# Experts' input of the last five blocks: block transposes on VectorE and a trip through DRAM in place of TensorE transposes

## The chip, the cores and the metric

The kernel runs on one core of one Trainium2 chip. The metric is device time of one execution in microseconds (us). The kernel before takes 1170.67 us (median of 3 runs, 1169.65 to 1171.47). The engines are named as in the profile: PE (TensorE), DVE (VectorE), ACT (ScalarE), POOL (GpSimd), SP (SyncE, whose queue issues every DMA here).

## The reference

The input x is 4096 tokens of 512 features, float32. Two sublayers follow, each of them `x + layernorm(f(layernorm(x)))`.

- Attention over 64 fixed latent keys: `Q = h Wq^T + bq` in 16 heads of 32; for each head and token 64 logits against the latent keys; the four largest go through a softmax and weight the latent vectors; `V = h Wv^T + bv` is added; the sum goes through `Wo` and `bo`. (K is computed by the reference and not used.)
- Experts: `up = h Wu^T`, `gate = h Wg^T`, `hidden = silu(up) * gate` (2048 wide), `out = hidden Wd^T`. The three matrices are ternary: each weight is rounded to -1, 0 or 1 times a scale of its matrix.

## The kernel before

**Tiling.** Tokens are taken in 8 blocks (b = 0 to 7) of 512, a block in 4 tiles (t) of 128 tokens. Features lie in 4 chunks (c or k) of 128. The 2048 expert columns are 16 chunks (e = 0 to 15) of 128; a loop over e within a loop over b is the frame of the whole kernel, and "chunk" below means one turn e of it.

**One chunk on PE.** `F.up("u", e)` (8 matmuls into the PSUM tile pu, line 676), `F.up("g", e)` (8 matmuls into pg, line 676), then `F.down(e - 1)` (8 matmuls into the four accumulators acc, line 719). In chunk 0 the down of the block before (chunk 15) stands in that place. Each expert matmul is done twice, on a high and a low part of the activations: the high part `hi` is the float32 value rounded to the type FP32R, the low part `lo` is what is left. The weights are ternary and exact. PSUM holds one pu and one pg.

**One chunk on ACT and DVE.** ACT: tanh of pu (line 685). DVE: silu (688). DVE: gate, h times pg (693). ACT: hi (704). DVE: lo (709), which `F.down(e)` of the next chunk reads with hi.

**The pieces in between.** While block b's experts run, the attention of block b + 1 is computed in pieces. `pieces(A, after)` writes by hand in which chunk and place each piece is emitted: `put(e, k, f, ...)`, where place 3 is between up-u and tanh, 0 between tanh and silu, 1 between up-g and gate, 2 between down(e - 1) and lo. The scheduler is off (`tc.manual_schedule()`), so each engine runs its instructions in just this order. `after` is the attention of block b + 2, whose input is prepared at the end of block b.

The pieces of a block's attention A, in the kernel before:

- `a_stats`, `a_rstd`, `a_apply` (chunks 10 and 11): first layernorm, on the tiles `xa` loaded by `load_normed` in chunk 6. `a_blocks(c)` (11, place 2): for each feature chunk c, four DVE transposes of 128x128 (line 317; DVE's transpose turns each 32x32 square by itself) into a tile `za`, and a DMA to the DRAM tile `da` (321). `a_load` (15, place 2): four DMAs from `da` to `hT` (326), which put the squares where a full transpose would have them. In `hT` the tokens of each square row are in the order (c t i).
- `q` (chunks 1, 2, 4, 6; line 344), `l` (logits, 358), `m` (top 8, 376), `r` (384 to 388), `e` (exp, 393), `n` (399 to 404), `z` (transpose of the weights through DRAM, 411 to 419), `v` and `y` (431, 448), `o` (459), `o_bias`, `o_rstd`, `o_apply` (chunks 11 to 13): attention itself. q and v read `hT` through `taken(k)` and `ordered(k)`, patterns that pick tokens in the order they need.
- `f_stats`, `f_rstd` (13), `f_apply` (14): second layernorm, on DVE and POOL. `f_trans(t)` (tiles 0 and 1 at chunk 14 place 1, tiles 2 and 3 at chunk 15 place 0): `transpose_row` (282) does four PE transposes of 128x128 against `ident` into PSUM; ACT copies the result to `self.hi`, named hT_f (496); DVE subtracts it to give `self.lo`, named lT_f (497). These two are the operands `parts` of `Experts(b + 1)`: every up matmul reads all 512 tokens of one of them.

Buffers: hT, hT_f and the same of block b + 2 take turns in the place `X{b % 2}`; attnT and lT_f in `Y{b % 2}`. So `a_load` for block b + 2 waits until up-g of chunk 15 of block b has been read. Blocks 0 and 1 are prepared in a different way (class `FirstAttention`, with an order of its own at the start), block 2 (`SecondAttention`) with PE transposes for both layernorms' outputs.

At the end of a block: `y_stats` in chunk 0 of the next, `y_out` after silu of its chunk 1 (DVE, line 272, then POOL and the store).

Of the kernel before, what the change touches and what calls it, by code (L numbers as in the profile page):

```python
# [10 lines left out]
F32 = mybir.dt.float32  # L11
F32R = mybir.dt.float32r
BF16 = mybir.dt.bfloat16
AF = mybir.ActivationFunctionType
ALU = mybir.AluOpType
AX = mybir.AxisListType

P = 128
# [40 lines left out]
def latent_attention_ternary_glu(  # L59
# [15 lines left out]
    nc = tc.nc  # L75
    NT, D = x_in.shape
    E = wuT.shape[1]
    DC = D // P
    EC = E // P
    TB = 512  # L80
    TT = TB // P
# [5 lines left out]
    work = ctx.enter_context(tc.tile_pool(name="work", bufs=2))  # L87
    small = ctx.enter_context(tc.tile_pool(name="small", bufs=4))
    dram = ctx.enter_context(tc.tile_pool(name="dram", bufs=3, space=bass.MemoryType.DRAM))
# [16 lines left out]
    def transposed(which, b, name, dtype):  # L106
        return work.tile([P, DC, TB], dtype, tag=f"{which}{b % 2}", name=name, bufs=1)
# [7 lines left out]
    CH = E // 2  # L115
    halves = [(k, h) for k in range(DC) for h in range(2)]
    raw = {}
    late = []
    for q in range(DC):
        w = work.tile([P, D], F32, tag="xa", name=f"raw_d_6_{q}", bufs=TT)  # L120
        late.append(w)
    for n, i in RAW_ORDER:
        raw[n, i] = wpool.tile([P, CH], F32, tag="chunk", name=f"raw_{n}_{i}", bufs=6 * DC)
    for q in range(DC):
        raw["d", 6 + q] = late[q]
    count = {"u": 2 * DC, "g": 2 * DC, "d": 2 * DC + 2}

    def load_x(b):
# [8 lines left out]
    normed = {}  # L137

    def load_normed(b):
        for t in range(TT):  # L140
            xt = work.tile([P, D], F32, tag="xa", name=f"xa_{b}_{t}", bufs=TT)
            r = b * TB + t * P
            nc.sync.dma_start(out=xt, in_=x_in[r : r + P, :])
            normed[b, t] = xt

    def load_up(n, src):
        for i, (k, h) in enumerate(halves):
# [22 lines left out]
    for i in range(count["d"]):  # L170
        rows = 2 * P if i < 6 else P
        r = i * 2 * P if i < 6 else 12 * P + (i - 6) * P
# [21 lines left out]
    tern = {}  # L194
# [84 lines left out]
    def transpose_row(h, name):  # L279
        pt = at_psum(f"pt_{name}")  # L280
        for c in range(DC):
            nc.tensor.transpose(pt[:, c * P : (c + 1) * P], h[:, c * P : (c + 1) * P], ident)  # L282
        return pt.rearrange("p (c k) -> p c k", k=P)
# [3 lines left out]
    class Attention:  # L287
        def __init__(self, b):
            self.b = b
            self.hT = None  # L290
            self.attnT = None
            self.norm_a = Norm(f"a{b}")
            self.norm_o = Norm(f"o{b}")
            self.norm_f = Norm(f"f{b}")
            self.rows = {}
            self.qT, self.w, self.top, self.m8, self.left, self.wT, self.pv = ({} for _ in range(7))
            self.po = {}

        def a_stats(self, t):
            self.norm_a.stats(t, normed[self.b, t])

        def a_rstd(self, lo, hi):
            self.norm_a.rstd(lo, hi)

        def a_apply(self, t):
            self.norm_a.apply(normed[self.b, t], normed[self.b, t], t)

        def a_blocks(self, c):

            if c == 0:
                self.da = dram.tile([P, 4, DC, P], F32, tag="da", name=f"da_{self.b}", bufs=2)
            z = work.tile([P, 4, P], F32, tag="w", name=f"za_{self.b}_{c}", bufs=4)
            for t in range(TT):
                nc.vector.transpose(
                    z[:, :, 32 * t : 32 * t + 32],
                    normed[self.b, t][:, c * P : (c + 1) * P].rearrange("p (k j) -> p k j", j=32),
                )  # L320
            nc.sync.dma_start(out=self.da[:, :, c, :], in_=z)

        def a_load(self):
            self.hT = transposed("X", self.b, f"hT_{self.b}", F32)
            for k in range(4):
                nc.sync.dma_start(
                    out=self.hT[32 * k : 32 * k + 32, :, :],
                    in_=self.da.rearrange("(a j) k c e -> k j a (c e)", j=32)[k],
                )

        def taken(self, k):
            return self.hT.rearrange("p a (c e) -> p c a e", e=P)[:, k]

        def ordered(self, k):
            return self.hT.rearrange("p a (c t i) -> p c t a i", t=TT, i=32)[:, k]


        def q(self, c):  # L340
# [145 lines left out]
            self.rows["f", t] = row(f"h_f{self.b}_{t}")  # L486
            self.norm_f.apply(self.rows["f", t], x_tiles[self.b][t], t)

        def f_alloc(self):
            self.hi = transposed("X", self.b, f"hT_f{self.b}", F32R)  # L490
            self.lo = transposed("Y", self.b, f"lT_f{self.b}", F32R)

        def f_trans(self, t):
            src = transpose_row(self.rows.pop(("f", t)), f"f{self.b}_{t}")
            dst = self.hi[:, :, t * P : (t + 1) * P]
            nc.scalar.copy(dst, src)
            nc.vector.tensor_tensor(
                self.lo[:, :, t * P : (t + 1) * P], src, dst.bitcast(F32), ALU.subtract
            )

    class SecondAttention(Attention):
# [9 lines left out]
        def sorted(self, dst, src):  # L513
            return self.mixed(dst), src.rearrange("p (a t i) -> p a t i", t=TT, i=32)

        def a_apply(self, t):
            self.rows["a", t] = row(f"h_a{self.b}_{t}")
            self.norm_a.apply(self.rows["a", t], normed[self.b, t], t)

        def a_trans(self, t):  # L520
            if self.hT is None:
# [143 lines left out]
    class Experts:  # L665
# [6 lines left out]
        def up(self, n, e):  # L672
            p = ps_up.tile([P, TB], F32, tag=n, name=f"p{n}_{self.b}_{e}")
            for k in range(DC):
                for i, part in enumerate(self.parts):
                    nc.tensor.matmul(  # L676
                        p, lhsT=tern[n, 2 * k + e // 8][:, (e % 8) * P : (e % 8 + 1) * P], rhs=part[:, k, :],
                        start=(k == 0 and i == 0), stop=(k == DC - 1 and i == 1),
                    )
            (self.pu if n == "u" else self.pg)[e] = p  # L680
# [197 lines left out]
    def pieces(A, after):  # L878

        at = {(e, k): [] for e in range(EC) for k in range(4)}  # L880

        def put(e, k, f, *args):
            at[e, k].append(lambda: f(*args))

        if A.b > 1:
            if A.b == 2:
                put(0, 0, A.a_apply, 0)
                put(0, 0, A.a_apply, 1)
                put(0, 1, A.a_trans, 0)
                put(0, 1, A.a_trans, 1)  # L890
                put(0, 1, A.a_apply, 2)
                put(0, 1, A.a_apply, 3)
                put(0, 2, A.a_trans, 2)
                put(0, 2, A.a_trans, 3)
            put(1, 0, A.q, 0)
            put(2, 0, A.q, 1)
            put(4, 0, A.q, 2)
            put(6, 0, A.q, 3)
        put(1, 1, A.l, 0)
        put(2, 2, A.l, 1)  # L900
        put(5, 0, A.l, 2)
        put(7, 0, A.l, 3)
        for i in range(8):
            put(2 + i, 0, A.m, i)
            put(2 + i, 2, A.r, i)
            put(3 + i, 3, A.e, i)
            put(3 + i, 1, A.n, i)
            put(3 + i, 1, A.z, i)
        for c in range(DC):
            put(5 + 2 * c, 1, A.v, c)  # L910
            put(5 + 2 * c, 1, A.y, c)
        if after is not None and after.b == 2:
            put(14, 2, after.a_stats, 0)
            put(14, 2, after.a_stats, 1)
            put(15, 1, after.a_stats, 2)
            put(15, 1, after.a_stats, 3)
            put(15, 1, after.a_rstd, 0, 4)
        elif after is not None:
            put(10, 2, after.a_stats, 0)
            put(10, 2, after.a_stats, 1)  # L920
            put(11, 0, after.a_stats, 2)
            put(11, 0, after.a_stats, 3)
            put(11, 0, after.a_rstd, 0, TT)
            for t in range(TT):
                put(11, 1, after.a_apply, t)
            for c in range(DC):
                put(11, 2, after.a_blocks, c)
            put(15, 2, after.a_load)
        put(11, 2, A.o, 0)
        put(11, 2, A.o, 1)  # L930
        put(11, 2, A.o_bias, 0)
        put(12, 0, A.o, 2)
        put(12, 0, A.o_bias, 1)
        put(12, 0, A.o_rstd, 0, 2)
        put(12, 1, A.o, 3)
        put(12, 1, A.o_bias, 2)
        put(12, 2, A.o_apply, 0)
        put(12, 2, A.o_apply, 1)
        put(12, 2, A.o_bias, 3)
        put(12, 2, A.o_rstd, 2, 4)  # L940
        put(13, 0, A.o_apply, 2)
        put(13, 0, A.o_apply, 3)
        put(13, 1, A.f_stats, 0)
        put(13, 1, A.f_stats, 1)
        put(13, 1, A.f_rstd, 0, 2)
        put(13, 2, A.f_stats, 2)
        put(13, 2, A.f_stats, 3)
        put(13, 2, A.f_rstd, 2, 4)
        put(14, 0, A.f_apply, 0)
        put(14, 0, A.f_apply, 1)  # L950
        put(14, 1, A.f_alloc)
        put(14, 1, A.f_trans, 0)
        put(14, 1, A.f_trans, 1)
        put(14, 1, A.f_apply, 2)
        put(14, 1, A.f_apply, 3)
        put(15, 0, A.f_trans, 2)
        put(15, 0, A.f_trans, 3)
        return at

    prev = None  # L960
    for b in range(NB):
        if b > 0:
            A, nxt = nxt, after
        after = None
        F = Experts(b, (A.hi, A.lo))
        at = {}
        for e in range(EC):
            if e == 4 and 0 < b < NB - 1:
# [119 lines left out]
```

## Time and profile before

| | |
|---|---|
| median of 3 runs | 1170.67 us |
| the profiled execution | 1169.34 us |
| its span, first to last instruction | 1167.6 us, TensorE clock granted 0.997 |
| PE busy | 1147.7 us, 98% |
| DVE busy | 841.1 us, 72% |
| ACT busy | 368.7 us, 32% |
| POOL busy | 168.7 us, 14% |
| DMA | 80.38 MB, mean 69 GB/s |
| first up matmul of blocks 2, 3, 4, 5, 6, 7 | 364.33, 504.67, 645.02, 785.37, 925.71, 1066.06 us |

How to read it: blocks 3 to 6 begin 140.34 to 140.35 us apart, so one block stands for the others. Matmuls are pipelined: the duration of one (about 390 ns for a 128x512 expert matmul) is longer than the distance to the next, which is what counts for the time. Two successive expert matmuls start 0.227 us apart, so a chunk without pieces on PE takes 24 of them, 5.44 us.

### The profile page before, as it was taken

How to read it: one execution, taken by the hardware profiler on the slowest of the kernel's cores; microseconds unless marked ns; L12 is line 12 of the kernel's file. 1: busy time of each engine (PE TensorE's matmuls, PEld its weight loads, DVE VectorE, ACT ScalarE, POOL GpSimd, SP SyncE). 2: the span in 40 equal slices, each digit the busy share in tenths (PEclk: the TensorE clock that was granted, in tenths of full speed). 3: DMA queues.
4: the chain of work that ended last, by engine and by line, in shares of the span. 5: the costliest groups of instructions: out<-in, count | busy, mean ns of one | idle time of the engine just before them, and what ended most of it. 6: DMA issues, size and time to landing. Idle time of an engine off the chain costs nothing.

```text
span 1167.6 us, 14544 instructions
## 1 busy us (share of the span) xinstructions
PE 1147.7 (98%) x4730; PEld 784.6 (67%) x4730; DVE 841.1 (72%) x2981; ACT 368.7 (32%) x654; POOL 168.7 (14%) x205
## 2 busy tenths in 40 slices
PE   8999999999999999999999999999999999999997
PEld 5447665876757766676667766677665866657885
DVE  5975984868867778668786688766887768747335
ACT  4984541333213322133322232122331233212222
POOL 1066001310023000320003200032001220013000
PEclk9999999999999999999999999999999999999999
DMA  9700211023112231122220232211411112100000
GB/s 354 285 1 1 66 62 54 1 74 112 62 42 55 87 95 55 37 73 82 88 84 1 72 102 80 72 27 46 139 61 55 36 57 88 64 10 10 28 1 36
DMA packets 73323, 80.38 MB, mean 69 GB/s; under 512 B 7200, under 2 KB 46368, under 8 KB 73248
## 3 DMA queue, kind: packets, MB, share of 16 engines
q1 hardware_dynamic: 73248, 79.46, 20.8%
q8 instruction: 37, 0.61, 0.2%
q14 instruction: 38, 0.31, 0.1%
HBM read 51.12 MB, written 28.31 MB: 68 GB/s over the span
## 4 chain that ended last, share of the span: by engine, by line
PE 90%; DVE 7%; ACT 2%; issue 1%; DMA 0%; POOL 0%; SPq 0%; DVEq 0%; ACTq 0%
PE acc L719 19%; PE pg L676 19%; PE pu L676 19%; PE pv L431 8%; PE po L459 8%; PE pq L344 7%; PE pv L448 3%; PE pl L358 2%; PE pq L549 2%; DVE left L384 1%; PE pt_f L282 1%; DVE m L376 1%; PE po L632 1%; DVE w L404 1%; DVE w L386 1%
## 5 line engine op out<-in xcount | busy, mean ns | idle before, releaser
L676 PE MATMUL pg<-hT_f,tern_g 128*128 128x512 f32 x512 | 214.3, 419 | 0.0
L719 PE MATMUL acc<-tern_d,hi 128*128 128x512 f32 x512 | 207.7, 406 | 1.7 <-DVE y L272 1.7
L676 PE MATMUL pu<-hT_f,tern_u 128*128 128x512 f32 x512 | 203.7, 398 | 0.7 <-ACT hT_f L653 0.7
L719 PE MATMUL acc<-tern_d,lo 128*128 128x512 f32 x512 | 200.6, 392 | 0.1
L676 PE MATMUL pu<-lT_f,tern_u 128*128 128x512 f32 x512 | 199.7, 390 | 0.2 <-DVE lT_f L659 0.2
L676 PE MATMUL pg<-lT_f,tern_g 128*128 128x512 f32 x512 | 199.6, 390 | 0.0
L704 ACT CAST hi<-h 128x512 fp32r<-128x512 f32 x128 | 79.1, 618 | 258.3 <-DVE h L693 258.3
L685 ACT ACTIVATE h<-pu,columns 128x512 f32<-128x512 f32 x128 | 87.5, 683 | 225.2 <-PE pu L676 224.6
L688 DVE SCALAR_TENSOR_TENSOR h<-h,pu 128x512 f32<-128x512 f32 x128 | 86.7, 678 | 98.4 <-ACT h L685 98.4
L719 PEld LDWEIGHTS acc<-tern_d,hi 128*128 128x128 f32 x512 | 96.3, 188 | 46.7 <-issue 26.5
L709 DVE TENSOR_TENSOR lo<-h,hi 128x512 fp32r<-128x512 f32 x128 | 89.2, 697 | 52.3 <-ACT hi L704 52.3
L693 DVE TENSOR_TENSOR h<-h,pg 128x512 f32<-128x512 f32 x128 | 85.6, 669 | 42.3 <-PE pg L676 41.4
L676 PEld LDWEIGHTS pg<-hT_f,tern_g 128*128 128x128 f32 x512 | 96.2, 188 | 27.7 <-issue 7.2
L676 PEld LDWEIGHTS pg<-lT_f,tern_g 128*128 128x128 f32 x512 | 96.2, 188 | 25.7 <-issue 7.4
L676 PEld LDWEIGHTS pu<-hT_f,tern_u 128*128 128x128 f32 x512 | 96.4, 188 | 23.6 <-issue 1.7
L676 PEld LDWEIGHTS pu<-lT_f,tern_u 128*128 128x128 f32 x512 | 96.5, 188 | 21.7 <-issue 1.7
L719 PEld LDWEIGHTS acc<-tern_d,lo 128*128 128x128 f32 x512 | 96.5, 189 | 21.0 <-issue 1.7
L431 PE MATMUL pv<-hT,wv 128*128 128x512 f32 x224 | 100.8, 593 | 2.2 <-ACT w L366 2.1
L384 DVE MATCH_REPLACE8 left<-m,w 128x64 f32<-128x64 f32 x512 | 100.2, 209 | 0.0
L459 PE MATMUL po<-wo,attnT 128*128 128x512 f32 x224 | 99.5, 592 | 0.0
L344 PE MATMUL pq<-hT,wq 128*128 128x512 f32 x192 | 86.2, 592 | 0.0
L459 PEld LDWEIGHTS po<-wo,attnT 128*128 128x128 f32 x224 | 42.4, 189 | 45.2 <-issue 41.9
(130 smaller groups left out, 1310.0 us busy)
## 6 DMA issues: line engine op xcount, KB each, us to landing
dz<-z SPq DMA_DIRECT2D x56, 256.0 KB, 2.0
wT<-dz SPq DMA_DIRECT2D x224, 64.0 KB, 1.9
x<-in_x SPq DMA_DIRECT2D x32, 256.0 KB, 3.5
out_x<-x SPq DMA_DIRECT2D x31, 256.0 KB, 2.0
xa<-in_x SPq DMA_DIRECT2D x24, 256.0 KB, 3.2
da<-za SPq DMA_DIRECT2D x20, 256.0 KB, 2.8
hT<-da SPq DMA_DIRECT2D x20, 256.0 KB, 5.1
raw_u<-in_wuT SPq DMA_DIRECT2D x8, 512.0 KB, 8.5
```

The source lines that it names most:

```text
L344: nc.tensor.matmul(pq, lhsT=wq[:, k, c * P : (c + 1) * P], rhs=self.taken(k), start=(k == 0), stop=(k == DC - 1),)
L384: nc.vector.match_replace(left[:, g, :], m8[:, g, :], w[:, g, :], TAKEN)
L431: nc.tensor.matmul(self.pv[c], lhsT=wv[:, k, c * P : (c + 1) * P], rhs=self.ordered(k), start=(k == 0), stop=False,)
L448: nc.tensor.matmul(self.pv[c][pr * HP : (pr + 1) * HP, :], lhsT=lv[:, 2 * c + pr, :], rhs=self.wT.pop(2 * c + pr), start=False, stop=True, ...
L459: nc.tensor.matmul(self.po[t], lhsT=self.attnT[:, c, t * P : (t + 1) * P], rhs=wo[:, c, :], start=(c == 0), stop=(c == DC - 1),)
L676: nc.tensor.matmul(p, lhsT=tern[n, 2 * k + e // 8][:, (e % 8) * P : (e % 8 + 1) * P], rhs=part[:, k, :], start=(k == 0 and i == 0), stop=( ...
L685: nc.scalar.activation(self.h[e], self.pu[e], AF.Tanh, scale=half_u[0])
L688: nc.vector.scalar_tensor_tensor(self.h[e], self.h[e], 1.0, self.pu.pop(e), ALU.add, ALU.mult)
L693: nc.vector.tensor_tensor(self.h[e], self.h[e], self.pg.pop(e), ALU.mult)
L704: nc.scalar.copy(hi, self.h[e])
L709: nc.vector.tensor_tensor(lo, self.h.pop(e), self.hid[e][0].bitcast(F32), ALU.subtract)
L719: nc.tensor.matmul(self.acc[t], lhsT=part[:, t * P : (t + 1) * P], rhs=wd, start=(e == 0 and i == 0), stop=(e == EC - 1 and i == 1),)
```

## The change

For blocks 3 to 7 (`Attention` itself; blocks 0 to 2 keep PE transposes):

1. The second layernorm's output is no longer transposed on PE. `f_blocks(t)` does one DVE transpose of 128x512 per token tile into a tile `zf` (in the place "w") and writes it to a DRAM tile `far`; `f_load(half)` reads two token tiles at a time into a tile of its own, `whole` (named hw, in the place "xa"), by four DMAs; `f_split(t)` makes hi on ACT and lo on DVE out of `whole`. `f_apply` and `f_blocks` of all tiles are emitted in chunk 13 (tile 0 at place 0, tile 1 at place 1, tiles 2 and 3 at place 2), the two loads at chunk 13 place 2, and the splits in chunk 15: tile 0 at place 0, tiles 1 and 2 at place 1, tile 3 at place 2.
2. The first layernorm's output is transposed by token tile too: `a_blocks(t)` is one 128x512 transpose in place of four of 128x128. `hT` then holds its tokens in the order (t c i), and `taken` and `ordered` change with it.
3. The attention of these blocks, from `q` to `f_stats`, is emitted one chunk earlier (`s = 1`); `q(0)` moves from chunk 1 place 0 to chunk 0 place 2, `q(1)` from chunk 2 place 0 to chunk 1 place 1, `m(0)` from chunk 2 to chunk 1 place 1. The preparation of the block after next (`a_stats` to `a_blocks`) moves with it; `a_load` stays at chunk 15 place 2.
4. `xa` becomes one tile of four parts, loaded by one DMA of 1 MB in place of four of 256 KB; the last four pieces of the raw down weights, which use the same place at the start, become parts of one tile.

```diff
-        def a_blocks(self, c):
-            if c == 0:
-                self.da = dram.tile([P, 4, DC, P], F32, tag="da", name=f"da_{self.b}", bufs=2)
-            z = work.tile([P, 4, P], F32, tag="w", name=f"za_{self.b}_{c}", bufs=4)
-            for t in range(TT):
-                nc.vector.transpose(
-                    z[:, :, 32 * t : 32 * t + 32],
-                    normed[self.b, t][:, c * P : (c + 1) * P].rearrange("p (k j) -> p k j", j=32),
+        def blocks(self, which, t, h):
+            if t == 0:
+                self.far[which] = dram.tile(
+                    [P, 4, TT, P], F32, tag="far", name=f"far_{which}{self.b}", bufs=3
                 )
-            nc.sync.dma_start(out=self.da[:, :, c, :], in_=z)
+            z = work.tile([P, 4, P], F32, tag="w", name=f"z{which}_{self.b}_{t}", bufs=4)
+            nc.vector.transpose(
+                z.rearrange("p k (c i) -> p c k i", i=32),
+                h.rearrange("p (c k j) -> p c k j", k=4, j=32),
+            )
+            nc.sync.dma_start(out=self.far[which][:, :, t, :], in_=z)
+
+        def a_blocks(self, t):
+            self.blocks("a", t, normed[self.b][:, t, :])
...
         def taken(self, k):
-            return self.hT.rearrange("p a (c e) -> p c a e", e=P)[:, k]
+            return self.hT.rearrange("p a (t c i) -> p c a t i", t=TT, i=32)[:, k]
 
         def ordered(self, k):
-            return self.hT.rearrange("p a (c t i) -> p c t a i", t=TT, i=32)[:, k]
+            return self.hT.rearrange("p a (t c i) -> p c t a i", t=TT, i=32)[:, k]
...
+        def f_blocks(self, t):
+            self.blocks("f", t, self.rows.pop(("f", t)))
+
+        def f_load(self, half):
+            if half == 0:
+                self.whole = work.tile([P, 4, TB], F32, tag="xa", name=f"hw_{self.b}", bufs=1)
+            part = slice(2 * half * P, (2 * half + 2) * P)
+            for k in range(4):
+                nc.sync.dma_start(
+                    out=self.whole[32 * k : 32 * k + 32, :, part],
+                    in_=self.far["f"].rearrange("(a j) k t e -> k j a (t e)", j=32)[k][:, :, part],
+                )
+
+        def f_split(self, t):
+            if t == 0:
+                self.hi = transposed("X", self.b, f"hT_f{self.b}", F32R)
+                self.lo = transposed("Y", self.b, f"lT_f{self.b}", F32R)
+            src = self.whole[:, :, t * P : (t + 1) * P].rearrange("p a (c i) -> p c a i", i=32)
+            hi, lo = (
+                x[:, :, t * P : (t + 1) * P].rearrange("p c (a i) -> p c a i", i=32)
+                for x in (self.hi, self.lo)
+            )
+            nc.scalar.copy(hi, src)
+            nc.vector.tensor_tensor(lo, src, hi.bitcast(F32), ALU.subtract)
...
+        s = 1 if A.b > 2 else 0
...
+        elif A.b > 2:
+            put(0, 2, A.q, 0)
+            put(1, 1, A.q, 1)
+            put(3, 0, A.q, 2)
+            put(5, 0, A.q, 3)
...
+        if s:
+            for t in range(TT):
+                put(13, min(t, 2), A.f_apply, t)
+                put(13, min(t, 2), A.f_blocks, t)
+            put(13, 2, A.f_load, 0)
+            put(13, 2, A.f_load, 1)
+            for t in range(TT):
+                put(15, (t + 1) // 2, A.f_split, t)
+        else:
+            put(14, 0, A.f_apply, 0)
+            put(14, 0, A.f_apply, 1)
+            put(14, 1, A.f_alloc)
+            put(14, 1, A.f_trans, 0)
+            put(14, 1, A.f_trans, 1)
...
```

## The prediction

> **What bounds the kernel now.** I read the page first: busy times and the chain of waits.
>
> ```profile
> span 1167.6 us, 14544 instructions
> ...
> PE 1147.7 (98%) x4730; PEld 784.6 (67%) x4730; DVE 841.1 (72%) x2981; ACT 368.7 (32%) x654; POOL 168.7 (14%) x205
> ...
> PE 90%; DVE 7%; ACT 2%; issue 1%; DMA 0%; POOL 0%; SPq 0%; DVEq 0%; ACTq 0%
> ```
>
> PE is the bound. Next the busy times by stretch, for one block in the middle: PE is busy in all 132 us, DVE in 98.8.
>
> ```profile
> 500.00:632.00 132.00, 132.00 (x537) 89.00 (x536) 98.77 (x363) 34.69 (x64) 15.77 (x17) 1.00 0.23 72
> ```
>
> So whatever leaves PE is gained in full, and whatever makes PE wait is lost in full: no slack takes it up. The timeline of PE, chunk 15 of block 4, shows what the removed transposes cost there.
>
> ```profile
> 780.61 0.39 PE L676 MATMUL pu<-lT_f,tern_u 128*128 128x512 f32 x1
> 780.84 1.03 PE L282 MATMUL pt_f<-ident,h_f 128*128 128x128 f32 x8
> 781.63 0.48 PE L676 MATMUL pg<-hT_f,tern_g 128*128 128x512 f32 x1
> 781.94 0.39 PE L676 MATMUL pg<-lT_f,tern_g 128*128 128x512 f32 x1
> ```
>
> Eight transposes push the next matmul from 780.84 to 781.63, and slow the following ones a little. Then ACT and DVE in the same chunk, from their timelines, because the new work lands there.
>
> ```profile
> 781.10 0.69 ACT L685 ACTIVATE h<-pu,columns 128x512 f32<-128x512 f32 x1
> 781.68 1.06 ACT L496 CAST hT_f<-pt_f 128x512 fp32r<-128x512 f32 x2
> 785.00 0.62 ACT L704 CAST hi<-h 128x512 fp32r<-128x512 f32 x1 [2.25 <-DVE h L693]
> ```
>
> ```profile
> 782.29 1.29 DVE L497 TENSOR_TENSOR lT_f<-pt_f,hT_f 128x512 fp32r<-128x512 f32 x2 [0.55 <-ACT hT_f L496]
> 783.50 0.68 DVE L688 SCALAR_TENSOR_TENSOR h<-h,pu 128x512 f32<-128x512 f32 x1
> 784.28 0.69 DVE L693 TENSOR_TENSOR h<-h,pg 128x512 f32<-128x512 f32 x1
> ```
>
> Two lo in a row and the silu after them start 0.605 us apart ((783.50 - 782.29) / 2): that is DVE's step. All four lo are done before gate today, and the next block's first up starts at 785.37, unhindered.
>
> **What the change takes away.** Chunks 14 and 15 of block 4 last 6.34 and 6.33 us (first up matmul to first up matmul: 772.68, 779.02, 785.37) against 5.44 for a chunk of 24 expert matmuls: 0.90 + 0.89 = 1.79 us for 16 transposes. Five blocks: -8.95 us. The Trainium skill, "VectorE: DVE Perf Modes", section "The three transpose paths", gives 390 ns for one TensorE transpose; by it the 80 would be worth an estimated 31 us. The trace has 1.79 / 16 = 0.11 us each, so I stay with 8.95.
>
> **What it adds at the block's end.** The splits come in chunk 15 in this order. ACT: tanh, hi(0), hi(1), hi(2), high of chunk 15, hi(3). DVE: lo(0), silu, lo(1), lo(2), gate, lo(3), low of chunk 15. PE wants all of hi and lo when down(14) ends. With no transposes in the chunk that begins at 779.02, PE is through at 779.02 + 5.44 = 784.46. The chain, in the rows above:
> - tanh 781.10 as now (it waits for up-u); hi(0) from 781.68; lo(0) from 782.29, as the rows have it.
> - silu 782.90, lo(1) 783.50, lo(2) 784.11, gate 784.71 to 785.40: one DVE step each.
> - high of chunk 15 ends 0.62 + 0.05 later, 786.07; hi(3) half a step behind it, 786.58; lo(3) 786.61 to 787.30.
> - The first up matmul (hi) can start at 786.62, the second (lo) at 787.35, in place of 784.46 and 784.69: PE loses 2.66 us. What is queued behind it on PE is all that follows.
>
> Data can only add to this. In chunk 13 DVE starts f_apply(0) 2.34 us into the chunk (as in chunk 14 today: 775.02 against 772.68). Four applies (0.46 a step, line 272), four transposes (0.71, line 411), silu and gate follow, so zf(3) is done 8.4 us into chunk 13, at 779.02 - 10.88 + 8.4 = 776.6. The DMA rows:
>
> ```profile
> wT<-dz SPq DMA_DIRECT2D x224, 64.0 KB, 1.9
> ...
> da<-za SPq DMA_DIRECT2D x20, 256.0 KB, 2.8
> hT<-da SPq DMA_DIRECT2D x20, 256.0 KB, 5.1
> ```
>
> The write lands at about 779.4; the second half's four loads are issued until 780.7 (0.42 us each on SP). A load of 128 KB lies between 1.9 and 5.1 us; by bytes 3.0: landed 783.7, or 782.6 to 785.8. hi(2) must start by 783.5 not to delay lo(2). I take 0.1 us on top of 2.66, so 2.75 per boundary, and keep 0 to 2.3 for the range. The first half has been issued by 778.5 and is there for hi(0). Five boundaries: +13.75 us.
>
> **The clock after the wait.** The trace has one long PE wait in the steady part, in chunk 1 of block 7 (down waits for y_out), from PE's timeline; and the busy times by stretch around it and around an earlier wait.
>
> ```profile
> 1074.90 0.39 PE L676 MATMUL pg<-lT_f,tern_g 128*128 128x512 f32 x1
> 1076.96 0.47 PE L719 MATMUL acc<-tern_d,hi 128*128 128x512 f32 x1 [1.67 <-DVE y L272]
> ```
>
> ```profile
> 1074.57:1077.98 3.41, 1.74 (x8) 0.85 (x6) 2.39 (x4) 0.00 (x0) 2.36 (x3) 1.00 0.00 0
> 1077.98:1081.40 3.42, 3.42 (x9) 2.44 (x8) 2.54 (x4) 0.62 (x1) 3.42 (x4) 0.50 0.41 153
> 125.66:129.07 3.41, 2.13 (x10) 1.42 (x8) 3.38 (x22) 3.41 (x6) 0.00 (x0) 1.00 0.30 103
> ```
>
> The last column but two is the granted clock. A stretch of 3.41 us with 1.67 us idle is followed by 3.41 us at 0.50; one with 1.28 us idle (125.66) is not. The new wait is 2.66 us in matmul starts, 2.3 to 2.4 idle, and stretches of 3.41 us fall on it at any phase. With 1.67 as the limit both parts of 2.4 stay below it in 0.94 of 3.41 us (28%), with 1.28 in 5%: four of five boundaries lose 3.41 x 0.5 = 1.71 us of PE time. +6.8 us, with 0 and 8.5 as ends.
>
> A rule speaks against this term. The Trainium skill, "TensorE: Matmul & The Clock Gate", section "Why this matters for your kernels", warns of PE gaps above about 3 us only, one idle window giving half clock. By it this term would be 0 and the forecast an estimated 1176. The row of 1076.96 differs, and a measurement decides.
>
> **What moves.** q(0) of block 3 goes to chunk 0 of block 2. hT landed there at 370.46 (last load issued 363.82, landing 6.65 us later), and PE would reach q(0) at 364.33 + 5.44 = 369.77: +0.7 us, once. At the later boundaries hT lands 5.5 us after the old start while q(0) comes 5.44 + 2.7 us after it: nothing. If the boundary wait weren't there, it would cost 0.1 a block.
>
> Chunk 1 now holds y_out (four steps of 0.72), m(0) and r(0) on DVE, 9.5 us in a PE chunk of 10.2 (q and l lie in it): covered, by q(1). The tightest places today, gate in chunks 8 and 10, end 0.83 us before the next up-g; in chunks 7 and 9 the same sequence runs. In chunk 13, low ends 9.0 us in, down wants it at 9.3. I take nothing for the three; if the cover of the last is gone, 0.2 us a block.
>
> At no cost on the path: 16 small transposes of za (0.19 a step) become 4 of 0.63, and 4 of zf come in, +2.3 us of DVE per block; q's rhs is read in runs of 32 instead of 128, but pv already is and takes the same 592 ns (lines 431, 344); xa's single DMA has 25 us from chunk 6 to chunk 9, and 1 MB of wq took 8.2. SP issues 12 transfers more per block where it idles, none ahead of hT's loads that waits later than they do. POOL's rstd keeps its order.
>
> **Sum.** -8.95 + 13.75 + 6.8 + 0.7 = +12.3 us, on the profiled execution of 1169.34 us (span 1167.6 and 1.7 around it): 1181.6. The median of the runs shown is 1.3 above that execution: 1183.0.
>
> **The rivals.**
> - *The boundary wait is hidden (faster).* If hi(3) and lo(3) are ready when down(14) ends, only -8.95 + 0.7 and 0.5 for hT remain: 1163. The chain from tanh to lo(3) would have to take 2.66 us less, for instance if SBUF-sourced lo and hi were much shorter than the PSUM-sourced rows; line 272, one SBUF input, has a step of 0.46 against 0.605, which over four lo yields 0.6, not 2.66. Against it too: the order on ACT and DVE is fixed. It decides in favour of faster below (8.95 - 0.7) / 5 = 1.65 us per boundary, clock included. 10%.
> - *The wait comes, the clock stays.* +5.5 us: 1176. For it: the limit lies between 1.28 and 1.67 on two cases only. 20%, for 1173 to 1179.
> - *Late data.* At 5.1 us per load hi(2) starts 2.3 us late: +11.5, and the longer gap gives half clock each time: 1196. For it: the loads follow each other on one queue, and hT's fourth took 6 us. 15% for 1188 and up.
> - Within 0.2% of no change, the wait being near 1.65: 5%.
>
> **Numbers.** A measurement of this kernel tells 0.2% (2.3 us) from no change. The forecast case has 50%, 1179 to 1188. The range of 8 in 10 takes in the case of the steady clock and half of the late data: 1174 to 1193. Faster 0.10, same 0.05, slower 0.85.
>
> **What would show it.** PE's timeline after each of the five boundaries: pu<-hT_f waiting about 2 us for ACT hT_f, then 0.5 for DVE lT_f; granted clock 0.5 for 3.4 us after most; chunks 14 and 15 at 5.44 us; block period near 143. Wrong if PE shows no idle time before pu, if ACT's hT_f waits for a DMA by more than 0.5 us (late data), or if other lines (q, down, y) show PE waits.

## The result, and the profile after

The changed kernel takes 1190.65 us (median of 4 runs, 1189.44 to 1191.17) against 1170.16 us (median of 4 runs of the kernel before): ratio 1.0179, 95% interval 1.0167 to 1.0191. It is 20.5 us slower. The prediction was 1183.0 us, 1174 to 1193, with 0.85 on slower: the direction and the mechanism held, and two of its terms were too small. The time lies above its forecast case (1179 to 1188, 50%), in the band that it gave to late data (1188 and up, 15%).

The profiled execution took 1190.26 us, its span 1188.2 us at a granted clock of 0.988. Its page, with the PE clock in 40 slices and the shares of the chain of waits:

```profile
span 1188.2 us, 14413 instructions
...
PE 1150.0 (97%) x4650; PEld 781.6 (66%) x4650; DVE 849.2 (71%) x2941; ACT 371.4 (31%) x654; POOL 168.5 (14%) x205
...
PEclk9999999999999999999999999989999999998999
...
PE 79%; DVE 11%; DMA 4%; ACT 3%; issue 2%; SPq 1%; POOL 0%; DVEq 0%; ACTq 0%
```

PE executes 80 instructions fewer, and is still busy for 2.3 us longer: some of its instructions run at half clock. The two 8s in the row of the clock are the slices with two stretches of it, of 3.41 us each. PE's share of the chain falls from 90% to 79%, and DVE, DMA and ACT take it over. What PE waits for, from the list of PE's waits (total us, times, longest):

```profile
PE pu L706 <- ACT hT_f L513: 16.2, 5, 3.9
...
PE acc L749 <- DVE y L268: 1.7, 1, 1.7
...
PE pq L345 <- DMA hT<-far_a: 0.9, 1, 0.9
```

The first row is new, five times, one for each boundary of the changed blocks (boundary b, 3 to 7, is the start of block b); the second is y_out's wait of before, and the third the one wait of q(0) for hT that was foretold. The beginning of block 4 shows what happens in such a boundary. ACT, DVE and PE, from their timelines (start, duration; in brackets the idle time before and who ended it); chunk 15 of block 3 begins at 642.01:

```profile
644.09 0.69 ACT L715 ACTIVATE h<-pu,columns 128x512 f32<-128x512 f32 x1 [1.98 <-PE pu L706]
645.20 1.14 ACT L513 CAST hT_f<-hw 128x512 fp32r<-128x512 f32 x2 [0.42 <-DMA hw<-far_f]
647.16 0.62 ACT L513 CAST hT_f<-hw 128x512 fp32r<-128x512 f32 x1 [0.82 <-DMA hw<-far_f]
649.13 0.62 ACT L734 CAST hi<-h 128x512 fp32r<-128x512 f32 x1 [1.36 <-DVE h L723]
649.66 0.61 ACT L513 CAST hT_f<-hw 128x512 fp32r<-128x512 f32 x1
```

```profile
645.85 0.69 DVE L514 TENSOR_TENSOR lT_f<-hw,hT_f 128x512 fp32r<-128x512 f32 x1 [3.02 <-ACT hT_f L513]
646.46 0.68 DVE L718 SCALAR_TENSOR_TENSOR h<-h,pu 128x512 f32<-128x512 f32 x1
647.05 1.45 DVE L514 TENSOR_TENSOR lT_f<-hw,hT_f 128x512 fp32r<-128x512 f32 x2
648.42 0.68 DVE L723 TENSOR_TENSOR h<-h,pg 128x512 f32<-128x512 f32 x1
650.30 0.69 DVE L514 TENSOR_TENSOR lT_f<-hw,hT_f 128x512 fp32r<-128x512 f32 x1 [1.20 <-ACT hT_f L513]
```

```profile
647.23 0.39 PE L749 MATMUL acc<-tern_d,lo 128*128 128x512 f32 x1
650.32 0.54 PE L706 MATMUL pu<-hT_f,tern_u 128*128 128x512 f32 x1 [2.71 <-ACT hT_f L513]
651.05 0.80 PE L706 MATMUL pu<-lT_f,tern_u 128*128 128x512 f32 x1 [0.19 <-DVE lT_f L514]
```

The order is the one that the prediction wrote out: hi(3) behind high of chunk 15, that behind gate, that behind lo(2). What it hadn't is ACT's wait of hi(0) for `hw<-far_f` (0.42 us in its row); for the wait of hi(2) (0.82 us) it had put 0.1 us on top. hi(0) starts at 645.20, 3.19 us into the chunk; by the prediction it would be 2.66. lo(0), silu, lo(1), lo(2), gate and hi(3) all follow it, and the first two up matmuls come 2.87 + 0.50 us late (in starts: 650.32 - 647.23 - 0.227, and 651.05 - 650.32 - 0.227). At boundaries 3 to 7 this is 3.47, 3.37, 4.54, 3.58 and 4.55 us, 19.5 in all.

The DMA issues of 636 to 646 us, with the median from issue to landing:

```profile
hw<-far_f SPq DMA_DIRECT2D x8, 128.0 KB, 3.3
far_f<-zf SPq DMA_DIRECT2D x3, 256.0 KB, 2.5
```

Busy time by stretch around boundaries 4 and 5 (length, then PE, PEld, DVE, ACT, POOL; granted clock; DMA share; GB/s):

```profile
647.23:650.65 3.42, 0.71 (x3) 0.19 (x1) 2.15 (x4) 1.69 (x3) 0.00 (x0) 1.00 0.97 234
650.65:654.07 3.42, 3.23 (x8) 2.46 (x8) 0.95 (x2) 0.00 (x0) 0.00 (x0) 0.50 0.23 47
790.60:794.01 3.41, 0.49 (x3) 0.07 (x1) 2.73 (x5) 0.89 (x3) 0.00 (x0) 1.00 0.93 227
794.01:797.42 3.41, 2.44 (x5) 1.72 (x6) 1.29 (x2) 0.91 (x2) 0.00 (x0) 0.50 0.30 62
797.42:800.84 3.42, 3.42 (x9) 2.64 (x9) 0.69 (x1) 0.69 (x1) 0.00 (x0) 0.50 0.00 0
```

After every boundary the clock is halved for 3.41 us; after boundaries 5 and 7 for two stretches in a row. That makes seven stretches, in which PE is busy for 22.2 us and, at 0.50, does the work of 11.1.

**The account.** Transposes gone -8.95 us; boundary waits +19.5; half clock +11.1; the half clock in block 7 of before (at 1077.98), which this execution does not have, -1.7; q(0) of block 2, +0.9. The sum is +20.9; the spans differ by 20.6 (1188.2 - 1167.6).

### The profile page after: what moved, and what is told of

Read it like the earlier page. It is cut to its first block, busy times and chain, and to the rows that moved or that the text cites. A ratio compares the mean times of both kernels' runs of the same rounds, so it can differ in the third digit from the quotient of the medians.

```text
span 1188.2 us, 14413 instructions
## 1 busy us (share of the span) xinstructions
PE 1150.0 (97%) x4650; PEld 781.6 (66%) x4650; DVE 849.2 (71%) x2941; ACT 371.4 (31%) x654; POOL 168.5 (14%) x205
## 4 chain that ended last, share of the span: by engine, by line
PE 79%; DVE 11%; DMA 4%; ACT 3%; issue 2%; SPq 1%; POOL 0%; DVEq 0%; ACTq 0%
PE pu L706 17%; PE pg L706 16%; PE acc L749 16%; PE pv L432 8%; PE po L460 8%; PE pq L345 7%; PE pv L449 2%; PE pl L359 2%; PE pq L579 2%; DMA hw<-far_f 1%; DVE left L385 1%; DMA far_f<-zf 1%; DVE h L723 1%; DVE st_f L241 1%; DVE m L377 1%
## 5 line engine op out<-in xcount | busy, mean ns | idle before, releaser
L706 PE MATMUL pu<-hT_f,tern_u 128*128 128x512 f32 x512 | 209.4, 409 | 16.9 <-ACT hT_f L513 16.2
L706 PE MATMUL pu<-lT_f,tern_u 128*128 128x512 f32 x512 | 204.6, 400 | 0.9 <-DVE lT_f L514 0.7
```

The source lines that it names most:

```text
L706: nc.tensor.matmul(p, lhsT=tern[n, 2 * k + e // 8][:, (e % 8) * P : (e % 8 + 1) * P], rhs=part[:, k], start=(k == 0 and i == 0), stop=(k = ...
```

## The experiments

The theory after the result: (a) the order of the splits costs about 2.7 us at each boundary even with the data there, (b) late data adds to that, (c) idle PE halves its clock. The rivals are that data alone makes the wait, and that the slow up matmuls have another cause than the idle time. Each run is compared with runs of the kernel before on the same chip (1169.4 to 1170.2 us). All edits are to the changed kernel unless another is named; `...` in a fence stands for lines left out.

**Data that is always there.** The splits read a weight tile of the same shape in SBUF; the loads into `hw` go on. The experts then compute on other numbers, so this kernel serves for its time alone.

```diff
-            src = self.whole[:, :, t * P : (t + 1) * P].rearrange("p a (c i) -> p c a i", i=32)
+            src = wq[:, :, t * P : (t + 1) * P].rearrange("p a (c i) -> p c a i", i=32)
```

> The splits read the resident weight tile wq in place of the loaded tile hw, so that no split waits for data; transposes, writes and loads stay (the experts then compute on other numbers). Theory A (order): the chain of hi, lo, silu, gate in chunk 15 alone keeps PE waiting 2.66 us at each of five boundaries (13.3 us against 19.5 in the changed kernel, counted in matmul starts), and each wait gives one stretch of half clock: 1181 us. Theory B (data alone): the late loads make the wait, and without them it goes away: 1163 us.

Measured: 1182.33 us, ratio 1.0108 (1.0085 to 1.0132). PE's waits, and its busy time by stretch around boundaries 3 and 5:

```profile
PE pu L706 <- ACT hT_f L513: 10.1, 5, 2.0
```

```profile
504.19:507.60 3.41, 1.40 (x5) 0.95 (x6) 1.85 (x3) 1.14 (x2) 0.00 (x0) 1.00 1.01 228
507.60:511.01 3.41, 3.41 (x10) 2.64 (x9) 0.69 (x1) 0.69 (x1) 0.00 (x0) 0.50 0.10 22
787.49:790.90 3.41, 2.43 (x11) 1.69 (x9) 3.09 (x5) 1.29 (x4) 0.00 (x0) 1.00 0.68 182
790.90:794.31 3.41, 2.15 (x8) 1.57 (x9) 1.29 (x2) 0.98 (x2) 0.00 (x0) 1.00 0.88 189
```

With no data to wait for, each boundary costs 2.18 + 0.50 = 2.68 us in starts, five times alike; the prediction's chain of ACT and DVE steps gave 2.66. So (a) holds with its size, and data alone is not the cause. The clock is halved after four of the five. After boundary 5 it is not: the same wait is cut by the edge of a stretch (790.90) into 0.98 and 1.26 us of idle time. (One more half clock, from 1091.28, follows y_out's wait in block 7.) What is left to the changed kernel, 1190.65 - 1182.33 = 8.3 us, is the price of late data with the clock that follows it.

**The order undone.** All four splits before gate of chunk 15, with the true data.

```diff
-                put(15, (t + 1) // 2, A.f_split, t)
+                put(15, 1, A.f_split, t)
```

> All four splits are emitted in chunk 15 at place 1, before gate, and the data path stays. Theory A (order, with data as the second limit): hi(3) no longer stands behind gate and high; what remains is the landing of the second half, about 5.1 us into chunk 15 (5.9 at two boundaries), then hi(2), hi(3), lo(3): PE waits 1.4 us at three boundaries and 2.3 at two, with half clock at those two at most: 1172 us, 1169 to 1174. Theory B (data alone): the order is of no account and the time stays near 1190 us.

Measured: 1175.34 us (1.0043; 1.0029 to 1.0056), a little above its range. PE's waits, and the two stretches at half clock:

```profile
PE pu L706 <- ACT hT_f L513: 6.0, 5, 1.5
...
PE acc L749 <- DVE y L268: 1.7, 1, 1.7
PE pu L706 <- DVE lT_f L514: 1.6, 5, 0.3
```

```profile
788.63:792.04 3.41, 3.41 (x10) 2.64 (x9) 1.34 (x2) 0.69 (x1) 0.00 (x0) 0.50 0.12 25
...
1082.18:1085.59 3.41, 3.41 (x10) 2.44 (x9) 2.46 (x4) 0.62 (x1) 3.41 (x4) 0.50 0.41 154
```

The boundaries now cost 2.07, 1.56, 2.18, 1.69 and 2.20 us in starts (9.7 in all, half of 19.5), and the clock is halved after one of them, boundary 5; the stretch from 1082.18 comes 12.7 us after the start of block 7 and follows y_out's wait, as in the kernel before. hi(2) now waits for `hw`, whose last part lands 5.2 to 5.75 us into the chunk, just when PE is through at 5.44. The wait that the order made is gone, and the data is what comes last.

**Both.** All splits before gate, and from the weight tile (so again on other numbers).

> Both edits together: all splits before gate, and read from wq. Theory A: four lo at 0.61 us a step after silu end 5.9 us into chunk 15; PE waits 0.3 us per boundary and the clock stays full: 1164 us (the removed transposes, 8.95 us, less 0.9 for q(0) of block 3 and 1 to 2 for the rest). Rival C (the moved attention or the DVE load costs something too): 1168 us or more, with PE waits at other lines.

Measured: 1164.14 us (0.9951; 0.9933 to 0.9969). A boundary costs 0.28 us, and after none is the clock halved. The three runs split the loss: without order and data the change would be worth -6.1 us (1164.14 against 1170.21); the order costs 18.2 (1182.33 - 1164.14); the data 8.3 on top. Taken the other way round, late data without the order costs 11.2 (1175.34 - 1164.14) and the order 15.3 on top (1190.65 - 1175.34): each hides a part of the other, so neither has one price, but the order is the larger in both.

**The wait filled.** Twelve matmuls that nobody reads stand on PE behind down(14), so that it is busy while it would wait.

```diff
+        def f_fill(self):
+            p = at_psum(f"fill_{self.b}")
+            for i in range(12):
+                nc.tensor.matmul(
+                    p, lhsT=tern["u", 0][:, :P], rhs=tern["d", 0][:, :TB], start=(i == 0), stop=(i == 11)
+                )
...
+            put(15, 2, A.f_fill)
```

> The changed kernel with 12 matmuls of no use (0.227 us each, 2.7 us) on PE between down(14) and the next block's first up, in the time in which PE waits. Theory A with the clock: the wait stays as it is, but no stretch of 3.41 us holds 1.67 us of idle time, so the granted clock stays 1.0 at all five boundaries: 9 to 11 us less than the changed kernel, 1180 us. Rival D (the half clock costs nothing, since it falls on waiting time or is made up later): 1190 us.

Measured: 1183.17 us (1.0106; 1.0083 to 1.0129), 7.5 us less than the changed kernel, although the operands come as late as there (19.7 us in all). Expected were 9 to 11. PE's timeline at the start of block 4 and the stretch around it:

```profile
648.37 2.88 PE L519 MATMUL fill<-tern_d,tern_u 128*128 128x512 f32 x12
651.23 0.50 PE L713 MATMUL pu<-hT_f,tern_u 128*128 128x512 f32 x1
651.96 0.49 PE L713 MATMUL pu<-lT_f,tern_u 128*128 128x512 f32 x1 [0.23 <-DVE lT_f L514]
```

```profile
649.41:652.80 3.39, 3.16 (x14) 2.09 (x13) 1.89 (x3) 1.14 (x2) 0.00 (x0) 1.00 0.92 194
```

No boundary is followed by half clock; a single stretch of it, at 131.26, lies in block 1, which the change doesn't touch. So (c) holds: it is the idle time that halves the clock, since late operands alone do not, and PE work that computes nothing is worth 7.5 us here, an estimated 9 without that one stretch (1.7). It doesn't pay for the wait.

**The chunk forward and the token order by themselves.** The second layernorm is transposed by PE again (`f_alloc` and `f_trans` in `Attention`, emitted as before); the attention stays a chunk forward and the first layernorm in token order.

```diff
-        if s:
+        if False:
             for t in range(TT):
                 put(13, min(t, 2), A.f_apply, t)
```

> The changed kernel with the second layernorm's output transposed on PE again, at the old places (chunks 14 and 15); token-order blocks, the single xa load and the attention one chunk forward stay. Theory A (all of the loss comes from the path through DRAM to the splits): the waits before pu<-hT_f and the half clock after them go, and the transposes' 8.95 us come back; what is left is 0.9 us for q(0) of block 3 and up to 0.4 us at each of four later boundaries, where q(0) now comes 5.4 us after the block's start and hT about as late: 1171 to 1173 us. Rival C (moving the attention forward costs by itself, through the fuller chunk 1 or the gates): 1175 us or more, with PE waits at pg, acc or pv.

Measured: 1172.45 us (1.0022; 1.0012 to 1.0033). PE's waits show where it goes:

```profile
PE pq L345 <- DMA hT<-far_a: 1.4, 2, 0.8
```

q(0) stands behind the down of chunk 0 and is wanted 5.44 us after the block's start; hT lands at 6.02, 5.5, 6.1, 5.54 and 5.59. The blocks are 0.3 to 1.0 us longer than before. In the changed kernel the boundary wait had covered this; "if the boundary wait weren't there, it would cost 0.1 a block" was too low.

The next kernel puts the attention back in its old chunks as well, so that of the change only the token order and the single load of `xa` are left.

```diff
-        s = 1 if A.b > 2 else 0
-        if A.b == 2:
+        s = 0
+        if A.b >= 2:
```

> As the one with PE transposes, and the attention back at its old chunks: of the change only the token-order blocks of the first layernorm and the single load of xa are left. Theory A: no work on PE differs and no wait is added: 1170 us, within 1 us of the kernel before. Rival C: if this one is already slower, the patterns by which q and v read hT cost PE time.

Measured: 1169.25 us, ratio 1.000 (0.9989 to 1.001), with blocks of 140.34 to 140.35 us as before. No cost of these parts is seen, within 0.1%, as predicted.

**Fewer tiles through DRAM.** Late data can be had earlier by having less of it. Tiles 0 to 2 go through DRAM, tile 3 through PE in chunk 14; all splits before gate. `f_load` now takes the first tile of a load and the one after its last, and tile 2 has loads of its own.

```diff
-                put(13, min(t, 2), A.f_blocks, t)
-            put(13, 2, A.f_load, 0)
-            put(13, 2, A.f_load, 1)
-            for t in range(TT):
-                put(15, (t + 1) // 2, A.f_split, t)
+                if t < 3:
+                    put(13, min(t, 2), A.f_blocks, t)
+            put(13, 2, A.f_load, 0, 2)
+            put(13, 2, A.f_load, 2, 3)
+            put(14, 0, A.f_alloc)
+            for t in range(3, TT):
+                put(14, 1, A.f_trans, t)
+            for t in range(3):
+                put(15, 1, A.f_split, t)
```

> Tiles 0 to 2 of the second layernorm's output go through DRAM, tile 3 by four PE transposes in chunk 14; the third tile has loads of its own (64 KB each), and all three splits stand in chunk 15 before gate. Theory A: 60 transposes of 0.11 us leave PE (-6.7 us); the third tile lands about 3.6 us into chunk 15, its lo ends at 4.9, before PE is through at 5.4: no wait, 0.9 us for q(0) of block 3 and up to 1 for the others: 1165 to 1166 us. Theory B (loads of this path are late whatever their number): a wait of 1 us or more at the boundaries stays: 1170 us or more.

Measured: 1165.13 us, ratio 0.9963 (0.995 to 0.9975): faster than both kernels. With four tiles in the same order of splits it was 1175.34, so this gain is that of the count. `hw` lands 2.07 to 3.75 us into chunk 15, the last lo ends at 5.3 to 5.6, and PE shows no wait at a boundary. With two tiles through DRAM and two through PE:

> Tiles 0 and 1 through DRAM, tiles 2 and 3 by PE transposes in chunk 14. Theory A: 40 transposes leave PE (-4.5 us), the two tiles have landed about 3 us into chunk 15, no wait: 1167 to 1168 us, slower than with three tiles by 2. Theory B: as late as the others, 1170 us or more.

Measured: 1168.01 us (0.9986; 0.9977 to 0.9995). Against all tiles on PE (1172.45) the first two bring 4.4 us, the third 2.9, and the fourth, by 1175.34, loses 10.

**q(0) a place later.** In the kernel of three tiles q(0) still met hT (blocks of 139.3 to 139.5 us after the first). It goes to place 0 of chunk 1, with l(0) and then q(1) at place 1.

```diff
-            put(0, 2, A.q, 0)
+            put(1, 0, A.q, 0)
+            put(1, 1, A.l, 0)
             put(1, 1, A.q, 1)
...
-            put(1, 0, A.l, 0)
```

> The three-tile version with q(0) back in chunk 1 place 0 (as before the change) and l(0) behind it in place 1; the rest of the attention stays a chunk forward. Theory A: hT has landed by then at every boundary, the wait before pq (0.8 us at block 2, 0.1 to 0.3 at the others, 1.6 to 2 in all) goes, nothing new waits: 1163 us. Rival C (l(0) and m(0) now come too late, and DVE is late for the gates): 1165 us or more, with a PE wait at pg or pl.

> The version with all transposes on PE, with q(0) back in chunk 1 as above. Theory A: the 2.6 us (0.22%) that it lost to the kernel before were hT's late landing at q(0) (1.0, 0.2, 0.8, 0.2 and 0.3 us of PE time at five boundaries); they go: 1169.5 to 1170.5 us, the same as before. Rival C (the fuller chunk 1 costs): 1172 us.

Both missed: 1166.37 us (0.9969; 0.9958 to 0.998) and, on the kernel with all transposes on PE, 1173.12 (1.0025; 1.0014 to 1.0036). PE's waits of the first:

```profile
PE pq L345 <- ACT w L367: 3.4, 5, 0.7
```

The wait for hT is gone, and a new one stands in its place: q(1) directly behind l(0) needs a place in PSUM, of which there are two, that ACT's copies of l(0)'s logits give free. So q(1) was put one place later, behind down(0):

```diff
-            put(1, 1, A.q, 1)
+            put(1, 2, A.q, 1)
```

> As e9_three_tiles_q_later, but q(1) stands one place later in chunk 1, after down(0), so that l(0)'s two PSUM copies by ScalarE have a chunk's work to finish in. Theory: both the wait of q(0) for hT and the wait of q(1) for a PSUM place (0.7 us in each of five blocks) are gone, and nothing new waits: about 1163 us (1161 to 1164.5). Rival: the attention, pushed later, meets another wait of the same size, and the time stays at 1165 us or above, with that wait named in the list of waits.

> The same edit on e10_pe_transposes_q_later: all transposes by TensorE, the attention a chunk forward, q(0) at the first place and q(1) at the third of chunk 1. Theory: what the chunk forward cost (1172.5 against 1169.4) was the wait of q(0) for hT alone, so the time is that of the kernel before, 1169.5 to 1170.5 us. Rival: 1172 us or above, with a wait of the attention at another place.

Measured: 1163.63 us, ratio 0.9955 (0.9939 to 0.9971), and 1169.07 (0.9997; 0.9983 to 1.001). The second shows that the chunk forward cost nothing but these waits. The first is the fastest version found, though its interval overlaps that of the three tiles before it. Its page, from an execution of 1160.84 us, the fastest of its six, and PE at the start of block 3:

```profile
span 1159.1 us, 14440 instructions
...
PE 1139.9 (98%) x4670; PEld 776.9 (67%) x4670; DVE 846.3 (73%) x2936; ACT 370.8 (32%) x654; POOL 168.6 (15%) x205
```

```profile
502.44 0.39 PE L747 MATMUL acc<-tern_d,lo 128*128 128x512 f32 x1
502.67 0.39 PE L704 MATMUL pu<-hT_f,tern_u 128*128 128x512 f32 x1
502.89 0.39 PE L704 MATMUL pu<-lT_f,tern_u 128*128 128x512 f32 x1
```

The up matmuls follow the down at 0.23 us, without a gap, and the blocks are 139.04 us apart against 140.34: 1.30 us for 12 transposes, at 0.11 us each.

## Why the prediction was right or wrong

- **Transposes, -8.95 us: right.** Chunk 14 lasts 5.44 us, PE is through with chunk 15 after 5.44, and three tiles' worth measured 1.30 us a block, as 0.11 us each gives. (The 390 ns that the prediction set beside it is the skill page's figure for a bf16 transpose; these are of float32.)
- **The order of the splits, 2.66 us: right.** With data always there it was 2.68.
- **Late data, 0.1 us a boundary: the step that failed.** By the trace it was 0.81, 0.71, 1.88, 0.92 and 1.89 us (the boundary's cost less 2.66), so the term of 2.75 measured 3.9. The working took 3.0 us for a load of 128 KB and concluded that "the first half ... is there for hi(0)". That had 0.2 us to spare (issued by 778.5, landing 781.5, wanted at 781.68), and a load took 3.1 to 3.7 us at boundary 4. Its four loads landed up to 2.96 us into the chunk instead of 2.48, hi(0) started 0.53 late, and everything behind it on ACT and DVE with it. The rest came from the second half, landing at 5.12 where by the prediction 4.5 would have done (its own landing, 783.7 for a start wanted by 783.5, gives 0.2 and not 0.1). The bound of 0 to 2.3 contained it; the value within was wrong, because only the second half had been given a bound. One of the signs that the prediction named for being wrong is there: hT_f waits for a DMA by more than 0.5 us (0.82 in ACT's row of 647.16).
- **Boundaries 5 and 7 were later by another microsecond.** At 5, the write of tile 1 took 4.34 us to land in place of 2.55, and the loads, which SP issues behind it, began 0.8 us late; at 7, the loads took up to 4.2 us and one held SP's queue for 1.6. The page counts 37 packets on the queue for instructions; one fell into the time of the late write, and one began as the load that held the queue was issued. In all these traces four writes of `zf` took over 4 us and each had such a packet in its time, while of 121 without one the longest took 3.5 us. That is no proof: 30 more writes had one and took at most 3.3, and loads of up to 4.6 us (with the wait filled, boundary 5) had none. The cause was not tried and stays open.
- **Half clock, +6.8 us: right in kind, too small.** It was sized for a wait of 2.66 us. With that wait (data always there) it came after four of five boundaries, as predicted; at 3.4 to 4.6 us it came after all five and twice for two stretches. 11.1 us in place of 6.8; the longer waits cost twice.
- **q(0), +0.7 us: right** (0.9). The margins in chunks 7, 9 and 13 held too: 0.84 us before up-g, and 0.37 before down where 0.3 was written.
- **Not foreseen:** the half clock of before in block 7 did not come back, -1.7 us. That is luck, since in some runs it comes there and in others not (last section); with it the time would be an estimated 1192, still in the range. The other misses add 5.8 us (late data), 4.3 (half clock) and 0.2 (q(0)).
- **The rivals.** The hidden wait is excluded for this order; its 1163 us was what the change is worth once order and data are out of the way (1164). The steady clock is excluded by the windows and by the filled wait. Late data was real, at about a third to four fifths of its 2.3 us per boundary, and it and the order worked together; the measured time lies in that rival's band.

## What to carry to other kernels

Work taken off the engine that bounds a kernel pays only if its replacement arrives when that engine wants it: add up the whole chain (queue of the issuing engine, write, load, and each step in program order on the engines behind it), and give every link a bound, also the link that seems to have time. A hand-written order couples engines that share no data: here one late load delayed silu and gate of another piece, and through them the next operand. Where the new path is too slow by a little, moving part of the work (three tiles of four) can gain where moving all of it loses.

## What the runs showed of the hardware

- **A wait of half a stretch can halve PE's clock.** Stretches of 3.413 us lie on a grid that is fixed within a run. Over all these traces, a stretch at full clock with at most 1.40 us of PE idle time was never followed by half clock; with 1.52 us or more it was, but for five (1.64, three times 1.68, and 1.89 us). So between 1.5 and 1.9 us the idle time alone doesn't decide: y_out's wait in block 7, 1.67 or 1.68 us within one stretch, was followed by half clock in three traces (before among them, 1074.57 in the prediction) and not in three others. What does decide there stays open. The stretch with that wait, and the next, in the run of the token order alone:

```profile
1074.05:1077.47 3.42, 1.74 (x8) 0.91 (x6) 2.40 (x5) 0.02 (x1) 2.30 (x4) 1.00 0.00 0
1077.47:1080.88 3.41, 3.41 (x14) 2.23 (x14) 2.72 (x4) 0.62 (x1) 3.41 (x4) 1.00 0.41 154
```

Where the grid's edge cuts a wait, each part counts for its own stretch: with data always there, 0.98 and 1.26 us at 787.49 were not followed by half clock, and 2.24 us within one stretch (boundaries 6 and 7) were. So the same wait can cost 1.7 us or nothing. After the change y_out's wait is cut like that (2.65 and 2.51 us busy):

```profile
1094.39:1097.81 3.42, 2.65 (x12) 1.88 (x10) 2.33 (x7) 0.69 (x1) 1.88 (x3) 1.00 0.00 0
1097.81:1101.22 3.41, 2.51 (x8) 1.29 (x9) 3.41 (x5) 0.00 (x0) 2.57 (x3) 1.00 0.12 44
```

- **Half clock lasts one stretch, and a second where the halved stretch has idle time of its own.** It did with 0.97 us (794.01 above) and with 0.36 (the row below, behind a stretch in which PE did nothing), and not with 0.19 (650.65 above). These are three cases, and no limit can be read from them.

```profile
1084.15:1087.56 3.41, 3.05 (x7) 2.13 (x8) 1.29 (x2) 0.30 (x1) 0.00 (x0) 0.50 0.00 0
```

- The Trainium skill, "TensorE: Matmul & The Clock Gate", section "What's actually happening", says that the window is free-running, 3413 ns long; the grid agrees. Its section "Why this matters for your kernels" warns only of gaps above about 3 us. Here a gap of 1.67 us sufficed (the row of 1076.96 in the prediction), and the measurement decides.
- Eight loads of 128 KB, issued 0.5 us apart, each took 3.1 to 3.7 us at boundary 4, where the last landed 7.6 us after the write of the last block transpose was issued (from 2.5 us before the start of chunk 15 to 5.12 behind it).
